# Turning x for layer 1: from TensorE and ScalarE to VectorE's 32x32 blocks and DMAs

## The chip, the cores and the metric

The kernel runs on one core of a Trainium2 chip. The metric is the device time of the whole kernel in microseconds, the median of several executions. Everything is float32.

## What is computed

The input x holds 128 graphs of 128 nodes with 512 features each, and adj is one 128x128 adjacency matrix. Four layers follow each other, and each one ends in a residual sum and a layer norm over the features:

```
layer 0:  x = LN(x + (adj x) W0 + bias)
layer 1:  q = x Wq', k = x Wk', v = x Wv'          (' is the transpose)
          rel = adj' * (q k')                      (* element by element, per graph)
          rel = rel / norm of its row
          x = LN(x + rel v)
layer 2:  h = x W;  e = leaky(s1 + s2') * adj;  att = softmax(e)
          x = LN(x + elu(att h + beta h))          (s1, s2: h times the two halves of a)
layer 3:  A = adj x;  C = adj x + b;  x = LN(x + max over n' of relu(A[.., n'] + C - A))
```

The change touches layer 1 only. There the kernel uses (x Wq')(x Wk')' = (x (Wq' Wk)) x': it makes the product matrix m_qk of the two weights once, then M = x m_qk and the scores M x' for each graph. TensorE contracts over the partitions (the 128 rows in which the on-chip memory is organised), so x has to lie with its features on the partitions and its nodes along the free dimension. After layer 0 it lies the other way round. The turned copy is called xT, and making it is what is changed.

## The kernel before, in words

**Groups and tiles.** The 128 graphs are taken in 32 groups of G = 4. For a group, x lies as [128 nodes, 4 graphs, 512 features] (x1 after layer 0, x2 after layer 1, x3 after layer 2). xT lies as [128, K = 4, 512]: feature k*128 + p on partition p, and the 4 x 128 nodes of the group along the free dimension.

**Products.** The four large products of a group (y with W0, m with m_qk, v with Wv', z with W2) are each a 512x512x512 product. `product` (L338) does it in seven steps on blocks of half size instead of eight, in the order 1, 2, 6, 5, 7, 3, 4 (L289). Some steps use sums and differences of blocks of the left factor. For m and v these are made by `left_factors` (L293) with four GpSimd instructions that read xT and write s_x. Each step is four matmuls of 128x256 in the program (eight records in the profile, since a float32 matmul is recorded as two), and its result leaves PSUM by a ScalarE copy or a VectorE addition. The profile calls the PSUM tiles of these steps r_y, r_m, r_v and r_z.

**Order of the work.** Nothing is left to a scheduler. Each piece of work is emitted at a due time from the table at L231: the number is a slot within the work of a group, group g is shifted by 28 slots, and all pieces are sorted by time (L757) and emitted; each engine then runs its instructions in that order. A group's pieces span some 130 slots, so that pieces of four to five groups stand side by side on every engine. What matters around the change, in slots of group g:

- 16.8 on: `norm`'s apply, ScalarE writes the normalised x1 of layer 0.
- 21.4, 22.4, 23.4, 24.4: `turn(b)` (L443), once for each graph. TensorE transposes four 128x128 blocks of x1 into a PSUM bank (p_xT), and ScalarE copies the bank into xT.
- 25.3 to 26.8: GpSimd makes the sums s_x from xT.
- 28 to 34: the seven steps of m. The first two read xT, the third reads a sum. M is written into the tile tT by ScalarE and VectorE.
- 36.5 to 39.5: `scores`, M times xT into p_rel.
- 39.95 to 41.5: `masked`, then `turn_rel` and `move_rel` (L489, L498): the masked scores are themselves turned by VectorE in blocks of 32x32 into relB, and 16 DMAs, 4 source quarters by 4 target quarters of the partitions, put the blocks in place in relT. VectorE's transpose turns each 32x32 block where it stands; exchanging the blocks across partitions is left to the DMAs.
- 42 to 48: the seven steps of v, of which the first, second and last read xT. Slot 48 is thus the last reader of xT, and falls on slot 20 of the next group. The tile xT has one buffer (tag aT_x).
- 50.6 on: `attend`, relT times v into p_o.

On TensorE, the turn of group g stands between the steps of z_w (r_z) of group g-2 and the `attend` matmuls of group g-1.

**Buffers.** The tiles tT (M), v and c (the result of z_w in layer 2) take turns in three buffers with the tag "nat". The same three hold the weights wq, wk and wv at the start.

**The DMA queue.** All DMAs of the loop are issued by SyncE in one order: for each group, the 16 DMAs of move_rel, four stores of the result of group g-3, and one load of x. The program rotates through eight semaphores for them, so a DMA waits until the one eight before it has landed.

Of the kernel before, what the change touches and what calls it, by code (L numbers as in the profile page):

```python
# [8 lines left out]
FP = mybir.dt.float32  # L9
# [20 lines left out]
def kernel(  # L30
# [33 lines left out]
    pe, dve, act, pool = (InOrder(tc, e) for e in (nc.tensor, nc.vector, nc.scalar, nc.gpsimd))  # L64
    sync = InOrder(tc, nc.sync)
    B, N, D = x.shape
    P = 128
    assert N == P and D % P == 0
    K = D // P
    Q = P // 32  # L70
    H = D // 2
    G = 4
# [5 lines left out]
    work = ctx.enter_context(tc.tile_pool(name="work", bufs=1))  # L78
# [3 lines left out]
    def bank(name):  # L82
        return psum.tile([P, D], FP, tag="ps", name=name)
# [8 lines left out]
    x1, x2, x3 = {}, {}, {}  # L92
# [12 lines left out]
    bias_sb = const.tile([P, D], FP)  # L105
    nc.scalar.dma_start(bias_sb, on_all(bias0, D))

    wq_sb = work.tile([P, K, D], FP, tag="nat", name="wq_sb", bufs=3)
    nc.sync.dma_start(wq_sb, wq.rearrange("(k p) f -> p k f", p=P))
    wk_sb = work.tile([P, K, D], FP, tag="nat", name="wk_sb", bufs=3)  # L110
    nc.sync.dma_start(wk_sb, wk.rearrange("(k p) f -> p k f", p=P))
    wv_sb = work.tile([P, K, D], FP, tag="nat", name="wv_sb", bufs=3)
    nc.sync.dma_start(wv_sb, wv.rearrange("(k p) f -> p k f", p=P))

    w2_sb = const.tile([P, K, D], FP)
# [104 lines left out]
    def emit(at, f, *args):  # L220
        pieces.append((at, lambda: f(*args)))

    def each(at, f):
        for b in range(len(at)):
            emit(at[b], f, b)

    def row(at, step, n=G):
        return [at + i * step for i in range(n)]
# [2 lines left out]
    TABLE = dict(  # L231
        load=[-20], y=row(0.5, 1), bias=row(1.3, 1), y_sums=row(5.2, 0.5), y_w=row(7, 1, 7),
        stats0=row(14.4, 0.4), norm0=[16.2], apply0=row(16.8, 0.33),
        turn=row(21.4, 1), x_sums=row(25.3, 0.5), m=row(28, 1, 7), scores=row(36.5, 1),
        masked=[39.95], squares=[40.4], turn_rel=[40.3],
        move_rel=row(41.2, 0.1), inverse=[42.5], v=row(42, 1, 7), attend=row(50.6, 1),
        residual=row(51.0, 1), dots=row(54.2, 1.1), norm1=[55.2], scale=[58.8],
# [6 lines left out]
        stats3=[99.8, 101.1, 104.7, 105.7], norm3=[106.2], apply3=row(107, 0.33), store=[108.5],  # L244
    )

    FIRST = {1: dict(y=row(-9.5, 0.3), bias=row(-9.2, 0.3))}

    LAST = {
        NG - 3: dict(  # L250
# [14 lines left out]
            m=[0.0, 1.73, 3.46, 5.2, 7.4, 9.1, 10.8], scores=row(12.7, 0.9), masked=[16.4],  # L265
# [16 lines left out]
    def times(g):  # L282
        t = {key: [28.0 * g + v for v in at] for key, at in TABLE.items()}
        t.update({key: [28.0 * g + v for v in at] for key, at in FIRST.get(g, {}).items()})
        t.update({key: [LAST_M + v / SLOT for v in at] for key, at in LAST.get(g, {}).items()})
# [7 lines left out]
    def left_factors(at, s, aT, tag, name, keep):  # L293

        def blk(nh, kh):
            return s[aT][:, 2 * kh : 2 * kh + 2, 2 * P * nh : 2 * P * (nh + 1)]

        def first():  # L300
            sums = work.tile([P, 3 + keep, 2, 2 * P], FP, tag=tag, name=f"s_{name}")
            s1, s2, s4 = (sums[:, i] for i in range(3))
            s3 = sums[:, 3] if keep else blk(1, 0)
            s["f"] = {1: blk(0, 0), 2: blk(0, 1), 3: s4, 4: blk(1, 1), 5: s1, 6: s2, 7: s3}
            pool.tensor_tensor(s1, blk(1, 0), blk(1, 1), ALU.add)

        emit(at[0], first)
        emit(at[1], lambda: pool.tensor_tensor(s["f"][6], s["f"][5], blk(0, 0), ALU.subtract))
        emit(at[2], lambda: pool.tensor_tensor(s["f"][7], blk(0, 0), blk(1, 0), ALU.subtract))
        emit(at[3], lambda: pool.tensor_tensor(s["f"][3], blk(0, 1), s["f"][6], ALU.subtract))  # L310
# [129 lines left out]
    def layer1(g, t):  # L440
        s = {}

        def turn(b):  # L443
            if b == 0:
                s["xT"] = work.tile([P, K, G * P], FP, tag="aT_x", name=f"xT_{g}")
            p = bank(f"p_xT_{g}_{b}")
            for k in range(K):
                pe.transpose(
                    p[:, k * P : (k + 1) * P], x1[g][:, b, k * P : (k + 1) * P], ident
                )  # L450
            act.copy(
                s["xT"][:, :, b * P : (b + 1) * P], p.rearrange("p (k n) -> p k n", k=K)
            )

        def begin_middle():
            s["tT"] = work.tile([P, K, G * P], FP, tag="nat", name=f"tT_{g}", bufs=3)

        def middle_block(nh, ch):
            return s["tT"][:, 2 * ch : 2 * ch + 2, 2 * P * nh : 2 * P * (nh + 1)]
# [48 lines left out]
            pool.tensor_tensor(s["rn"], s["n2"], mhalf, ALU.pow)  # L508

        def begin_values():  # L510
            s["v"] = work.tile([P, G, D], FP, tag="nat", name=f"v_{g}", bufs=3)

        def attend(b):
            s["o", b] = bank(f"p_o1_{g}_{b}")
# [37 lines left out]
        def scale_dots():  # L552
# [11 lines left out]
            )  # L564
            s12[g] = s["d"]

        each(t["turn"], turn)
        left_factors(t["x_sums"], s, "xT", "s_x", f"x_{g}", 1)
        product(t["m"], f"m_{g}", by_columns, s, "m", middle_block, True, begin_middle)
        each(t["scores"], scores)  # L570
        emit(t["masked"][0], masked)
        emit(t["squares"][0], squares)
        emit(t["turn_rel"][0], turn_rel)
        each(t["move_rel"], move_rel)
        emit(t["inverse"][0], inverse)
        product(t["v"], f"v_{g}", by_rows, s, "v", rows_of(lambda: s["v"]), True, begin_values)
        each(t["attend"], attend)
        each(t["residual"], residual)
# [9 lines left out]
    def layer2(g, t):  # L588
        s = {}
# [77 lines left out]
            )  # L667

        def begin():
            s["c"] = work.tile([P, G, D], FP, tag="nat", name=f"c_{g}", bufs=3)  # L670
            for b in range(G):
                s["c", b] = s["c"][:, b, :]

# [26 lines left out]
        n = G // len(t["exps"])  # L700
# [9 lines left out]
        if g < NG - 1:  # L710
            left_factors(t["z_sums"], s, "zT", "s_yz", f"z_{g}", 0)
            product(t["z_w"], f"z_{g}", by_rows, s, "2", rows_of(lambda: s["c"]), True, begin)
        else:
            each(t["z_w"], direct)
# [39 lines left out]
    for g in range(NG):  # L754
        for layer in (layer0, layer1, layer2, layer3):
            layer(g, times(g))
# [31 lines left out]
```

All engines are called through a helper (L26) that keeps program order, so that the profile puts nearly every instruction on line 26. The tile names tell them apart.

## Time and profile before

| | before |
|---|---|
| time, median of 3 | 2263.68 us (2263.55 to 2263.74) |
| span of the profiled execution | 2260.3 us |
| TensorE matmul, busy | 2221.2 us, 98% |
| VectorE, busy | 1599.1 us, 71% |
| ScalarE, busy | 1043.4 us, 46% |
| GpSimd, busy | 924.4 us, 41% |
| p_xT matmuls | 512, busy 76.1 us, mean 273 ns |
| copies p_xT to xT on ScalarE | 128, busy 74.5 us, mean 586 ns |
| TensorE clock granted | 0.996 |

The trace names an instruction by what it writes and reads: "p_xT<-ident,x" is a matmul into the PSUM tile p_xT from x and the identity matrix. A row of groups gives the instruction's count, its busy time, the mean duration of one in ns, and then the idle time of the engine just before such instructions with what ended it. A row of the timeline gives start, duration, engine, instruction and count; a bracket at its end is the idle time before it. PE is TensorE's matmul, PEld its loading of weights, DVE VectorE, ACT ScalarE, POOL GpSimd, SPq the queue of SyncE. Matmuls are pipelined, so their durations overlap, and what a matmul holds the engine for is the distance between two starts. A row of windows gives the busy time of each engine in a stretch, then the granted clock, the mean busy share of the 16 DMA engines and GB/s.

### The profile page before, as it was taken

How to read it: one execution, taken by the hardware profiler on the slowest of the kernel's cores; microseconds unless marked ns; L12 is line 12 of the kernel's file. 1: busy time of each engine (PE TensorE's matmuls, PEld its weight loads, DVE VectorE, ACT ScalarE, POOL GpSimd, SP SyncE). 2: the span in 40 equal slices, each digit the busy share in tenths (PEclk: the TensorE clock that was granted, in tenths of full speed). 3: DMA queues.
4: the chain of work that ended last, by engine and by line, in shares of the span. 5: the costliest groups of instructions: out<-in, count | busy, mean ns of one | idle time of the engine just before them, and what ended most of it. 6: DMA issues, size and time to landing. Idle time of an engine off the chain costs nothing.

```text
span 2260.3 us, 31788 instructions
## 1 busy us (share of the span) xinstructions
PE 2221.2 (98%) x11553; PEld 1884.2 (83%) x11553; DVE 1599.1 (71%) x3414; ACT 1043.4 (46%) x2056; POOL 924.4 (41%) x743
## 2 busy tenths in 40 slices
PE   7999999999999999999999999999999999999996
PEld 5888888888888888888888888888888888888873
DVE  4657776667766767766767766677767677667678
ACT  2235444454444454444454444544444544444545
POOL 3434444334444334444334443444443344443322
PEclk9999999999999999999999999999999999999998
DMA  4000111100111100111101111001111001110001
GB/s 164 24 24 9 40 39 42 43 24 25 43 38 43 42 24 25 41 40 43 43 12 37 39 42 43 24 24 43 38 43 43 25 24 42 39 43 24 15 15 56
DMA packets 79853, 83.67 MB, mean 37 GB/s; under 512 B 43985, under 2 KB 44113, under 8 KB 79697
## 3 DMA queue, kind: packets, MB, share of 16 engines
q1 hardware_dynamic: 78496, 79.28, 10.5%
q10 hardware_dynamic: 1200, 2.36, 0.3%
q8 instruction: 92, 1.51, 0.3%
q14 instruction: 65, 0.52, 0.1%
HBM read 39.65 MB, written 33.55 MB: 32 GB/s over the span
## 4 chain that ended last, share of the span: by engine, by line
PE 93%; DVE 4%; POOL 1%; ACT 1%; issue 1%; DMA 0%; ACTq 0%; DVEq 0%; POOLq 0%
PE r_y L26 17%; PE r_v L26 16%; PE r_m L26 16%; PE r_z L26 16%; PE p_rel L26 5%; PE p_z L26 5%; PE p_o L26 5%; PE p_y L26 5%; PE p_a L26 5%; PE p_xT L26 2%; DVE x L26 1%; DVE st L26 1%; PE p_eT L26 1%; PE p_m L26 1%; PE p_s L26 1%
## 5 line engine op out<-in xcount | busy, mean ns | idle before, releaser
L26 ACT ACTIVATE x<-x,nmean,rstd 128x512 f32<-128x512 f32 x512 | 389.0, 808 | 127.4 <-DVE nmean L26 127.2
L26 DVE BATCH_NORM_STATS2 st<-x 128x6 f32<-128x512 f32 x512 | 352.2, 688 | 74.8 <-ACT x L26 66.0
L26 POOL TENSOR_TENSOR rstd<-ve,mhalf 128x4 f32<-128x4 f32 (+1 forms) x134 | 144.5, 1078 | 360.0 <-DVE ve L26 356.0
L26 POOL TENSOR_TENSOR x<-x,bias_sb 128x512 f32<-128x512 f32 x128 | 173.9, 1361 | 146.5 <-PE p_y L26 146.5
L26 DVE SCALAR_TENSOR_TENSOR scr<-x,wa 128x512 f32<-128x512 f32 x256 | 214.4, 888 | 0.0
L26 ACT ACTIVATE x<-x,top 128x512 f32<-128x512 f32 x128 | 92.4, 722 | 225.3 <-DVE top L26 225.1
L26 DVE TENSOR_TENSOR v<-r_v,v 128x512 f32<-128x512 f32 x96 | 65.8, 685 | 178.5 <-PE r_v L26 175.5
L26 POOL TENSOR_TENSOR s_x<-xT 128x512 f32<-128x512 f32 x64 | 82.1, 1282 | 223.1 <-ACT xT L26 223.1
L26 DVE TENSOR_TENSOR x<-r_y,x 128x512 f32<-128x512 f32 x224 | 151.7, 678 | 30.2 <-PE r_y L26 29.8
L26 ACT COPY yT<-p_y 128x512 f32<-128x512 f32 x128 | 75.2, 587 | 205.7 <-PE p_y L26 205.7
L26 DVE SCALAR_TENSOR_TENSOR x<-p_o,rn,x 128x512 f32<-128x512 f32 x128 | 95.9, 749 | 100.0 <-PE p_o L26 97.1
L26 DVE SCALAR_TENSOR_TENSOR x<-m,x 128x512 f32<-128x512 f32 x128 | 114.8, 897 | 61.4 <-ACT m L26 51.4
L26 ACT COPY c<-r_z 128x512 f32<-128x512 f32 x124 | 72.7, 586 | 176.0 <-DVE scr L26 174.9
L26 PEld LDWEIGHTS p_y<-adjT,x 128*128 128x128 f32 x1024 | 135.0, 194 | 13.0 <-ACT adjT L26 5.1
L26 PE MATMUL p_y<-adjT,x 128*128 128x128 f32 x1024 | 135.8, 277 | 6.3 <-ACT adjT L26 4.8
L26 PEld LDWEIGHTS p_z<-eT,x 128*128 128x128 f32 x1024 | 133.9, 192 | 8.4 <-DVE x L26 1.2
L26 PEld LDWEIGHTS p_rel<-xT,tT 128*128 128x128 f32 x1024 | 134.1, 191 | 7.4 <-DVE tT L26 0.8
L26 PE MATMUL p_rel<-xT,tT 128*128 128x128 f32 x1024 | 134.9, 275 | 0.6 <-DVE tT L26 0.6
L26 PE MATMUL p_z<-eT,x 128*128 128x128 f32 x1024 | 134.8, 275 | 0.4 <-DVE x L26 0.4
L26 PE MATMUL p_a<-x,adjT 128*128 128x512 f32 x256 | 131.2, 597 | 3.6 <-ACT x L26 1.9
L26 ACT COPY tT<-r_m 128x512 f32<-128x512 f32 x128 | 75.7, 591 | 123.7 <-PE r_m L26 123.7
L26 POOL TENSOR_TENSOR s_z<-zT 128x512 f32<-128x512 f32 x31 | 39.2, 1263 | 225.7 <-ACT zT L26 225.7
(118 smaller groups left out, 5119.0 us busy)
## 6 DMA issues: line engine op xcount, KB each, us to landing
out_dram<-x SPq DMA_DIRECT2D x128, 256.0 KB, 2.0
x<-in_x_dram SPq DMA_DIRECT2D x31, 1024.0 KB, 5.3
relT<-relB SPq DMA_DIRECT2D x512, 16.0 KB, 1.8
w_sb<-in_L_gnn_weight_dram ACTq DMA_DIRECT2D x1, 1024.0 KB, 5.8
x<-in_x_dram SPq DMA_DIRECT2D x4, 256.0 KB, 7.7
wq_sb<-in_L_gnn_Wq_dram SPq DMA_DIRECT2D x1, 1024.0 KB, 12.2
wk_sb<-in_L_gnn_Wk_dram SPq DMA_DIRECT2D x1, 1024.0 KB, 14.9
w_sb<-in_L_gnn_W_dram ACTq DMA_DIRECT2D x1, 1024.0 KB, 10.1
```

The costliest lines, as they stand in the source:

```text
L26: return lambda *args, **kw: self.tc.keep_in_program_order(op(*args, **kw))
```

## The change

From the third group on, xT is made without TensorE and ScalarE. `turn_blocks(b)` at slots 18.4, 19.0, 19.6 and 20.2 turns one graph's x1 with one VectorE transpose in blocks of 32x32 into a new tile xB, laid out so that the values of one destination run are contiguous. `move(a)` at slots 20.5 to 20.8 issues 16 DMAs, each from 32 partitions of xB to 32 partitions of xT, in runs of 32 values, 128 bytes, 16 runs for each partition. The readers of xT (the sums, m, scores and v) are the same. It is for taking the transposes off TensorE. Groups 0 and 1 are turned as before, group 0 with its four pieces closer together.

xB needs a buffer of 8 KB a partition. It is found by letting M (tT) and v share one buffer (tag "tv"), with one buffer for c and one for xB: three in all, as before. The weights wq, wk and wv lie in these three at the start.

```diff
-    wq_sb = work.tile([P, K, D], FP, tag="nat", name="wq_sb", bufs=3)
+    wq_sb = work.tile([P, K, D], FP, tag="tv", name="wq_sb")
...
-        turn=row(21.4, 1), x_sums=row(25.3, 0.5), m=row(28, 1, 7), scores=row(36.5, 1),
+        turn=row(21.4, 1), turn_blocks=row(18.4, 0.6),
+        move=row(20.5, 0.1), x_sums=row(25.3, 0.5), m=row(28, 1, 7), scores=row(36.5, 1),
...
-    FIRST = {1: dict(y=row(-9.5, 0.3), bias=row(-9.2, 0.3))}
+    FIRST = {0: dict(turn=row(20.4, 0.3)), 1: dict(y=row(-9.5, 0.3), bias=row(-9.2, 0.3))}
...
+        def turn_blocks(b):
+            if b == 0:
+                s["xB"] = work.tile([P, Q, K, G, P // Q], FP, tag="xB", name=f"xB_{g}")
+                s["xT"] = work.tile([P, K, G * P], FP, tag="aT_x", name=f"xT_{g}")
+            dve.transpose(
+                s["xB"][:, :, :, b, :].rearrange("p q k u -> p k q u"),
+                x1[g][:, b, :].rearrange("p (k q u) -> p k q u", k=K, q=Q),
+            )
+
+        def move(a):
+            n = P // Q
+            for q in range(Q):
+                sync.dma_start(
+                    s["xT"][q * n : (q + 1) * n].rearrange("p k (b n) -> p (k b) n", b=G)[
+                        :, :, a * n : (a + 1) * n
+                    ],
+                    s["xB"][a * n : (a + 1) * n, q].rearrange("p k b n -> p (k b) n"),
+                )
...
-            s["tT"] = work.tile([P, K, G * P], FP, tag="nat", name=f"tT_{g}", bufs=3)
+            s["tT"] = work.tile([P, K, G * P], FP, tag="tv", name=f"tT_{g}")
...
-            s["v"] = work.tile([P, G, D], FP, tag="nat", name=f"v_{g}", bufs=3)
+            s["v"] = work.tile([P, G, D], FP, tag="tv", name=f"v_{g}")
...
-        each(t["turn"], turn)
+        if g < 2:
+            each(t["turn"], turn)
+        else:
+            each(t["turn_blocks"], turn_blocks)
+            each(t["move"], move)
...
-            s["c"] = work.tile([P, G, D], FP, tag="nat", name=f"c_{g}", bufs=3)
+            s["c"] = work.tile([P, G, D], FP, tag="c", name=f"c_{g}")
```

More of the change, by code (lines that the diff above doesn't have):

```diff
@@ L106 @@
     nc.scalar.dma_start(bias_sb, on_all(bias0, D))
-    wq_sb = work.tile([P, K, D], FP, tag="nat", name="wq_sb", bufs=3)
+    wq_sb = work.tile([P, K, D], FP, tag="tv", name="wq_sb")
     nc.sync.dma_start(wq_sb, wq.rearrange("(k p) f -> p k f", p=P))
-    wk_sb = work.tile([P, K, D], FP, tag="nat", name="wk_sb", bufs=3)
+    wk_sb = work.tile([P, K, D], FP, tag="c", name="wk_sb")
     nc.sync.dma_start(wk_sb, wk.rearrange("(k p) f -> p k f", p=P))
-    wv_sb = work.tile([P, K, D], FP, tag="nat", name="wv_sb", bufs=3)
+    wv_sb = work.tile([P, K, D], FP, tag="xB", name="wv_sb")
     nc.sync.dma_start(wv_sb, wv.rearrange("(k p) f -> p k f", p=P))
```

## The prediction

> **What bounds the kernel now.** I read the page's busy shares and its chain first, then the waits, then one group's timeline on TensorE and VectorE, last SyncE's queue and the DMA share.
>
> ```profile
> PE 2221.2 (98%) x11553; PEld 1884.2 (83%) x11553; DVE 1599.1 (71%) x3414; ACT 1043.4 (46%) x2056; POOL 924.4 (41%) x743
> ...
> PE 93%; DVE 4%; POOL 1%; ACT 1%; issue 1%; DMA 0%; ACTq 0%; DVEq 0%; POOLq 0%
> PE r_y L26 17%; PE r_v L26 16%; PE r_m L26 16%; PE r_z L26 16%; PE p_rel L26 5%; PE p_z L26 5%; PE p_o L26 5%; PE p_y L26 5%; PE p_a L26 5%; PE p_xT L26 2%; DVE x L26 1%; DVE st L26 1%; PE p_eT L26 1%; PE p_m L26 1%; PE p_s L26 1%
> ```
>
> The chain is TensorE for 93% of the span, and the turn of x (p_xT) is 2% of it. In the list of waits the longest entry of TensorE's matmuls is 4.8 us in total over the whole run. So time taken off TensorE comes back whole, unless something new makes TensorE wait. The chain's share is rounded; the timeline gives the price. On TensorE, a group in the middle of the run:
>
> ```profile
> 1039.28 1.89 PE L26 MATMUL r_v<-t_v,xT 128*128 128x256 f32 x8
> 1041.01 1.02 PE L26 MATMUL p_a<-x,adjT 128*128 128x512 f32 x2
> 1041.86 1.89 PE L26 MATMUL r_z<-w_sb,zT 128*128 128x256 f32 x8
> 1043.59 0.60 PE L26 MATMUL p_xT<-ident,x 128*128 128x128 f32 x4
> 1044.03 1.89 PE L26 MATMUL r_z<-w_sb,zT 128*128 128x256 f32 x8
> 1045.76 0.60 PE L26 MATMUL p_xT<-ident,x 128*128 128x128 f32 x4
> 1046.19 0.60 PE L26 MATMUL p_o<-v,relT 128*128 128x512 f32 x1
> ```
>
> The printed durations overlap, as matmuls are pipelined; what counts is start to next start. A block of four transposes holds TensorE from 1043.59 to 1044.03, 0.44 us.
>
> **What the Trainium skill says.** "TensorE: Matmul & The Clock Gate", Part 4 (PE-mode transpose), gives about 275 ns for a transpose in a kernel's context and says that the result lies in PSUM and has to be copied out. The trace agrees in both (273 ns mean for p_xT, and a ScalarE copy of 586 ns for each block), but the 273 ns is a latency: the spacing is 0.11 us. "VectorE: DVE Perf Modes", The three transpose paths, says that VectorE turns only 32x32 blocks, which is why DMAs must then put them in place, and it warns of plain DMAs that step through a transpose with a large innermost stride; here VectorE has made the innermost 32 values contiguous, so the warning is not this case. "DMA: Bandwidth & Descriptors" points two ways: its Specifications want at least 512 B for line rate, its section Why small descriptors are slow (HBM only) says that transfers within SBUF escape that, with 3 cycles of overhead for a packet: 11 cycles for 256 B. By that rule 128 B would be 128/32 + 3 = 7 cycles, an estimate. The trace of before has SBUF packets of 256 B and none of 128 B.
>
> **Removed.** For groups 2 to 31, 16 transposes on TensorE and 4 copies on ScalarE. TensorE: 4 blocks x 0.437 us = 1.75 us a group, x 30 groups = 52.4 us. ScalarE: 4 x 0.586 = 2.3 us a group; it is 46% busy and not on the chain, so I count 0. The four PSUM banks are freed too, worth 0 while nothing waits for banks.
>
> **Added on VectorE.** Four transposes of 128x512 a group. The row of the existing ones, 128x128, and of a pass over 128x512 in SBUF:
>
> ```profile
> L26 DVE STREAM_TRANSPOSE relB<-rel 128x128 f32<-128x128 f32 x128 | 28.7, 283 | 1.1
> ...
> L26 DVE BATCH_NORM_STATS2 st<-x 128x6 f32<-128x512 f32 x512 | 352.2, 688 | 74.8 <-ACT x L26 66.0
> ```
>
> A pass over 512 elements in SBUF takes 0.69 us (the statistics row), four times the small transpose 1.13 us; I take 0.7 us, as both are one pass over the tile. 4 x 0.7 = 2.8 us a group, at most 4.5. Do they fit? The instruction order of the changed program puts one ahead of the first v addition, two between the first and the second, one after "top". VectorE there:
>
> ```profile
> 1036.07 0.69 DVE L26 TENSOR_TENSOR v<-r_v,v 128x512 f32<-128x512 f32 x1 [3.91 <-PE r_v L26]
> 1038.62 0.69 DVE L26 TENSOR_TENSOR v<-r_v,v 128x512 f32<-128x512 f32 x1 [1.86 <-PE r_v L26]
> ...
> 1040.20 0.21 DVE L26 TENSOR_SCALAR top<-mx,b_sb 128x1 f32<-128x1 f32 x1
> 1041.27 0.69 DVE L26 BATCH_NORM_STATS2 st<-x 128x6 f32<-128x512 f32 x1 [0.85 <-ACT x L26]
> ```
>
> The brackets are idle time before the instruction: 3.91, 1.86 and 0.85 us, against 0.7, 1.4 and 0.7. They fit, and nothing queued behind them (the v additions, the statistics, the maxima) starts later. Cost 0. At 1.13 us each the second and third gap overrun by about 0.4 us, in a stretch where TensorE has no wait for VectorE; still 0 at first order. The last transpose ends at about 1041.1.
>
> **Added: the DMAs and the wait that replaces the copies.** Sixteen DMAs on SyncE's queue, each of 32 partitions x 16 runs of 128 B = 512 packets, 64 KB. The first may start only when its buffer is free: xT is single, and its last reader is r_v of the group before, which ends at 1041.01. So they start at about 1041.15, by TensorE and VectorE alike. TensorE needs all sixteen at the first r_m. It begins 18.15 us after the end of that r_v, 1059.16; less the 1.75 removed, 1057.4. The GpSimd sums s_x need them too, but r_m's first use of a sum is 5 us later and two sums take 2.6 us, so they tolerate a landing until about 1059.9. Window: 16.25 us. What is queued on SyncE behind the moves is four stores and one load with tens of us of slack. Is the window enough? The nearest thing measured is the move of the scores, also 16 DMAs from 32 partitions to 32 partitions in SBUF, 64 packets of 256 B each:
>
> ```profile
> 1021.71 10.18 SPq L26 DMA_DIRECT2D relT<-relB  x16
> ...
> relT<-relB SPq DMA_DIRECT2D x512, 16.0 KB, 1.8
> ...
> 1021.00:1032.00 11.00, 11.00 (x57) 9.17 (x56) 9.58 (x26) 5.59 (x16) 2.02 (x2) 1.00 0.10 22
> ...
> x<-in_x_dram SPq DMA_DIRECT2D x31, 1024.0 KB, 5.3
> ```
>
> First, issue. 10.18 / 16 = 0.64 us a DMA, set by the queue. Does issue grow with packets? The load of x is 512 packets in one DMA, and its issue takes 0.37 to 0.39 us on the queue's timeline. So it does not; I keep 0.64. Second, the engines. In the window row the DMA share is 0.10: 0.10 x 11 us x 16 engines = 17.6 us for 16 x 64 = 1024 packets, 17 ns a packet of 256 B. A 128 B packet lies between half of that, 8.5 ns, and all of it, 17 ns (the page's rule would make it 11). Sixteen moves are 8192 packets, 512 an engine: 4.4 to 8.7 us, all less than the issue, 10.2. So issue sets the pace: 15 x 0.64 + 2.0 for the last to land (1.8 for a small one, and the longer tail) = 11.6 us, landed at 1052.8. That is the time at which the fourth ScalarE copy ended before, and 4.6 us ahead of need. Cost 0. The bad end: if a 128 B packet cost two 256 B packets, 34 ns, 512 x 34 = 17.4, plus 2 = 19.4 us against 16.25: a stall of 3.2 us a group. The limit of "no stall" is 14.25 / 15 = 0.95 us a DMA; the gain is gone at (14.25 + 1.75) / 15 = 1.07 us.
>
> **The rest.** M and V in one buffer: V is first written when ScalarE copies r_v, 1024.70, after the scores read M, done by 1019; M of the next group is first written after 1060, after p_o has read V, done by 1056. Margins of over 4 us; cost 0. Group 0's turn emitted closer together and the weights in other buffers: only in the first 60 us; cost 0.
>
> **Sum.** 2263.7 - 52.4 + 0 = 2211.3 us.
>
> **Rivals.**
> 1. *DMAs too slow.* The r_m waits for the moves. With 34 ns a packet, a stall of 3.2 - 1.75 = 1.4 us net a group x 30 = +43: about 2307, slower than before. For: 245,760 packets of a size that no trace shows, the one page that asks for 512 B. Against: 17 ns at 256 B, and less to move per packet here.
> 2. *Gain partly eaten.* A pace of 1.0 us a DMA overruns by 15 x 0.05 = 0.75 us a group: 22 us back, 2234. For: issue of a pattern with sixteen short runs a partition is not measured either. Against: the load's issue of 0.38 us.
> 3. *Nothing left.* 1.07 us a DMA, or VectorE losing 1.75 us a group to TensorE's evacuations: 2264. Against: VectorE would rise only from 49.1 to 52 us in a group of 66.8, and the gaps are there.
>
> **How the numbers follow.** Forecast 0.70, rival 2 0.12, rival 3 0.04, rival 1 0.14. Faster by over 0.2%: 0.82; within: 0.04; slower: 0.14. Predicted 2211. The low end is 2205 (second-order help from free banks and ScalarE); the high end 2245 takes in most of rival 2 (up to 1.02 us a DMA). What is left out is rivals 1 and 3, some 0.2.
>
> **What would show it.** Right: no p_xT after the second group, group spacing 66.8 us in place of 68.6, moves issued at about 0.64 us, GpSimd's s_x released by a DMA at about the time it was released by the copy, and no wait of TensorE at r_m. Each step wrong: a list of waits with "r_m <- DMA", and then the queue's timeline says whether issue or packets set the pace; or VectorE's transposes well over 0.7 us and TensorE waiting for v or c. The prediction falls if the sixteen moves take over 16 us from first issue to last landing.

## The result, and the profile after

The changed kernel takes 2236.3 us (2235.4 to 2241.3) against 2263.6 us before (2263.3 to 2263.7): ratio 0.988, 95% interval 0.987 to 0.990. It is faster, but only by 27 us. The forecast was 52. The question is where the other 25 us went.

The page of the changed kernel: busy shares, the chain, the rows of VectorE's dot products (scr) and of GpSimd's sums, and the moves' row of DMA issues.

```profile
PE 2182.9 (98%) x11073; PEld 1842.1 (82%) x11073; DVE 1794.9 (80%) x3534; ACT 980.0 (44%) x1936; POOL 983.1 (44%) x743
...
PE 75%; DVE 20%; issue 3%; POOL 1%; ACT 1%; DMA 0%; DVEq 0%; ACTq 0%; POOLq 0%
...
L26 DVE SCALAR_TENSOR_TENSOR scr<-x,wa 128x512 f32<-128x512 f32 x256 | 286.2, 1169 | 0.0
...
L26 POOL TENSOR_TENSOR s_x<-xT 128x512 f32<-128x512 f32 x64 | 95.8, 1497 | 256.5 <-DMA xT<-xB 237.6
...
xT<-xB SPq DMA_DIRECT2D x480, 64.0 KB, 2.3
```

VectorE had 4% of the chain and now has 20%. It is busy for 196 us more (1794.9 against 1599.1), and the next lines show that the new transposes explain only 81 of them. The dots, which the diff does not touch, rose from 888 ns (214.4 us in all) to 1169 ns (286.2 us): 72 us. The first form of GpSimd's sums, also untouched, rose from 1282 ns to 1497 ns.

The new transposes, by shape, and then the waits that matter (waiting engine and tile, what it waits for: total us, times, longest):

```profile
L26 DVE STREAM_TRANSPOSE xB<-x 128x512 f32<-128x512 f32 x120 | 81.2, 696 | 38.6 <-ACT x L26 24.8 <-DMA relT<-relB 13.8
```
```profile
POOL s_x L26 <- DMA xT<-xB: 237.6, 29, 11.7
...
PE r_m L26 <- DVE tT L26: 6.8, 5, 1.7
...
PE r_y L26 <- DVE x L26: 4.4, 17, 0.4
```

In the loop no matmul waits for a DMA. TensorE waits for VectorE: r_m for the additions that build M, r_y for the additions x<-r_y,x that empty its PSUM tiles. The waits listed are short, 11.2 us in all, and do not add up to the 25 us, so the loss is better read from the distance between groups. From the start of one group's first r_m to the next it was 68.59 us in every group before. After, I sorted the groups of the trace (third to thirty-first) by that distance. "Lead" is how long before the first r_m the first sum s_x starts; "slow" counts those of VectorE's twelve instructions with both inputs in SBUF (eight dots, two x<-c,x and two x<-m,x, from 3 us before r_m to 20 us after) that took over 1 us instead of 0.68:

| | groups | lead, us | slow | first and second addition into M, us after r_m | distance, us |
|---|---|---|---|---|---|
| before | all | 6.0 | 3 | 5.5, 12.5 | 68.59 |
| after | 13 | 3.5 to 3.7 | 6 | 8.0 to 8.3, 12.5 | 66.81 |
| after | 8 | 3.3 to 3.5 | 7 | 8.3 to 8.5, 13.4 | 67.75 |
| after | 3 | 2.7 to 3.0 | 7 | 8.6 to 8.8, 13.6 | 67.9 to 68.2 |
| after | 4 | 2.2 to 2.5 | 8 to 9 | 9.0 to 9.3, 15.1 | 69.3 to 69.4 |
| after, the first with moves | 1 | 1.3 | - | - | 69.68 |

In 13 groups the whole forecast is there: 68.59 - 66.81 = 1.78 us. The others lose 8 x 0.94 + 3.7 + 10.0 + 2.9 = 24 us, which is the missing gain. The loss goes with the lead, and it goes in steps. In the eight groups that lose 0.94 us, TensorE loses nothing at r_m. Set beside a group without loss, it falls behind in r_y, 20.4, 28.3 and 30.5 us after r_m, and the wait that the trace names there is for x<-r_y,x. In the worst groups 1.5 us are lost at r_m and the rest in r_y.

Here is a group of the worst kind (r_m starts at 1046.32). First VectorE:

```profile
1044.68 1.08 DVE L26 SCALAR_TENSOR_TENSOR scr<-x,wa 128x512 f32<-128x512 f32 x1
...
1045.69 1.74 DVE L26 SCALAR_TENSOR_TENSOR scr<-x,wa 128x512 f32<-128x512 f32 x1
...
1049.12 1.75 DVE L26 SCALAR_TENSOR_TENSOR scr<-x,wa 128x512 f32<-128x512 f32 x1
...
1052.03 1.74 DVE L26 SCALAR_TENSOR_TENSOR scr<-x,wa 128x512 f32<-128x512 f32 x1
...
1053.70 1.75 DVE L26 SCALAR_TENSOR_TENSOR scr<-x,wa 128x512 f32<-128x512 f32 x1
...
1055.38 0.68 DVE L26 TENSOR_TENSOR tT<-r_m,tT 128x512 f32<-128x512 f32 x1
...
1057.06 1.81 DVE L26 SCALAR_TENSOR_TENSOR x<-c,x 128x512 f32<-128x512 f32 x1
1058.98 1.57 DVE L26 SCALAR_TENSOR_TENSOR x<-m,x 128x512 f32<-128x512 f32 x1
...
1061.40 0.67 DVE L26 TENSOR_TENSOR tT<-r_m,tT 128x512 f32<-128x512 f32 x1
```

Then GpSimd, and the matmul that waited for the second addition into M:

```profile
1043.95 1.27 POOL L26 TENSOR_TENSOR s_x<-xT 128x512 f32<-128x512 f32 x1 [8.92 <-DMA xT<-xB]
1045.29 1.60 POOL L26 TENSOR_TENSOR s_x<-s_x,xT 128x512 f32<-128x512 f32 x1
1046.85 1.73 POOL L26 TENSOR_TENSOR s_x<-xT 128x512 f32<-128x512 f32 x1
1048.53 1.79 POOL L26 TENSOR_TENSOR s_x<-xT,s_x 128x512 f32<-128x512 f32 x1
1050.28 1.46 POOL L26 TENSOR_TENSOR rstd<-ve,mhalf 128x4 f32<-128x4 f32 x1
1051.72 4.86 POOL L26 TENSOR_TENSOR x<-x,bias_sb 128x512 f32<-128x512 f32 x3
```
```profile
1062.13 1.99 PE L26 MATMUL r_m<-xT,t_m 128*128 128x256 f32 x8 [1.28 <-DVE tT L26]
```

And the same place before (r_m at 1059.16), GpSimd first:

```profile
1053.11 1.27 POOL L26 TENSOR_TENSOR s_x<-xT 128x512 f32<-128x512 f32 x1 [7.03 <-ACT xT L26]
...
1056.92 1.27 POOL L26 TENSOR_TENSOR s_x<-xT,s_x 128x512 f32<-128x512 f32 x1
```
```profile
1057.52 1.21 DVE L26 SCALAR_TENSOR_TENSOR scr<-x,wa 128x512 f32<-128x512 f32 x1
...
1058.66 0.68 DVE L26 SCALAR_TENSOR_TENSOR scr<-x,wa 128x512 f32<-128x512 f32 x1
```

Before, the four sums ended (1058.2) just as the dots began (1057.5), and met one of them. After, the sums start 2.4 us ahead of r_m and lie beside the dots. Each dot that meets one takes up to 1.75 us instead of 0.68, and the sums stretch too. GpSimd's next work, rstd, the additions of the bias and the sums s_y, then meets the later dots, x<-c,x and x<-m,x. VectorE runs in a fixed order, so the additions into M and the x<-r_y,x, which need no GpSimd, stand behind all that.

Most of the lost lead is the gain itself. Counted from the end of r_v, the sums start at 12.1 us before (1053.11 - 1041.01) and at 12.7 to 13.0 us after in most groups, so they are only 0.6 to 0.9 us later. But r_m, and the dots with it, starts at 16.38 us where it started at 18.15.

The steps can be read from one instruction, the first x<-m,x of a group. The last addition of the bias on GpSimd is released by TensorE, 10.72 us after r_m (11.03 in the first group with moves). First a group that loses nothing (r_m at 1519.50), then one that loses 0.94 us (r_m at 911.76):

```profile
1530.15 0.69 DVE L26 SCALAR_TENSOR_TENSOR x<-m,x 128x512 f32<-128x512 f32 x1
...
1530.22 1.75 POOL L26 TENSOR_TENSOR x<-x,bias_sb 128x512 f32<-128x512 f32 x1 [1.35 <-PE p_y L26]
```
```profile
922.48 1.27 POOL L26 TENSOR_TENSOR x<-x,bias_sb 128x512 f32<-128x512 f32 x1 [1.19 <-PE p_y L26]
...
922.57 1.74 DVE L26 SCALAR_TENSOR_TENSOR x<-m,x 128x512 f32<-128x512 f32 x1
```

The one that starts first runs its usual time, and the other pays. In the 13 groups without loss x<-m,x starts at most 0.003 us after that addition and takes 0.69 us. In the 16 others it starts at least 0.019 us after it and takes 1.56 to 1.80 us, and what follows on VectorE is late: the second addition into M comes at 13.4 us in place of 12.5. In the worst groups x<-c,x is already late enough to meet the addition (1057.06, 1.81 us), and x<-m,x meets the next sum as well. Before, x<-m,x starts 1.03 us ahead of the addition, and VectorE waits there for ScalarE. Stretched dots first use up this slack, and cost nothing until it is gone.

The Trainium skill names this: "SBUF — State Buffer", section Who interferes with whom, says that a VectorE instruction with two SBUF inputs contends with a GpSimd instruction that reads SBUF, that one with at most one SBUF input does not, and that the first to start keeps the shared ports for its whole instruction. The trace agrees: in the two pairs above the one that comes second pays, and for a dot 1.75 - 0.68 = 1.07 us is most of one 1.27 us sum. The additions into M read PSUM and one SBUF tile, and stay at 0.67 to 0.68 us in the worst group.

### The profile page after: what moved, and what is told of

Read it like the earlier page. It is cut to its first block, busy times and chain, and to the rows that moved or that the text cites. A ratio compares the mean times of both kernels' runs of the same rounds, so it can differ in the third digit from the quotient of the medians.

```text
span 2234.4 us, 31661 instructions
## 1 busy us (share of the span) xinstructions
PE 2182.9 (98%) x11073; PEld 1842.1 (82%) x11073; DVE 1794.9 (80%) x3534; ACT 980.0 (44%) x1936; POOL 983.1 (44%) x743
## 3 DMA queue, kind: packets, MB, share of 16 engines
q1 hardware_dynamic: 331936, 110.77, 19.6%
## 4 chain that ended last, share of the span: by engine, by line
PE 75%; DVE 20%; issue 3%; POOL 1%; ACT 1%; DMA 0%; DVEq 0%; ACTq 0%; POOLq 0%
PE r_v L26 17%; PE r_y L26 15%; PE r_z L26 14%; PE r_m L26 8%; DVE scr L26 6%; DVE x L26 6%; PE p_z L26 5%; PE p_o L26 5%; PE p_a L26 5%; PE p_rel L26 4%; DVE st L26 2%; PE p_y L26 2%; DVE tT L26 1%; DVE d L26 1%; PE p_m L26 1%
## 5 line engine op out<-in xcount | busy, mean ns | idle before, releaser
L26 DVE SCALAR_TENSOR_TENSOR scr<-x,wa 128x512 f32<-128x512 f32 x256 | 286.2, 1169 | 0.0
L26 POOL TENSOR_TENSOR x<-x,bias_sb 128x512 f32<-128x512 f32 x128 | 193.2, 1519 | 76.9 <-PE p_y L26 76.4
L26 POOL TENSOR_TENSOR s_x<-xT 128x512 f32<-128x512 f32 x64 | 95.8, 1497 | 256.5 <-DMA xT<-xB 237.6
L26 DVE SCALAR_TENSOR_TENSOR x<-m,x 128x512 f32<-128x512 f32 x128 | 129.7, 1013 | 13.6 <-DVE x L26 0.9
L26 PE MATMUL p_o<-v,relT 128*128 128x512 f32 x256 | 130.3, 593 | 0.0
## 6 DMA issues: line engine op xcount, KB each, us to landing
wq_sb<-in_L_gnn_Wq_dram SPq DMA_DIRECT2D x1, 1024.0 KB, 12.1
```

The lines of the kernel that those rows point to most:

```text
L26: return lambda *args, **kw: self.tc.keep_in_program_order(op(*args, **kw))
```

## The experiments

The theory, A: the sums start too late, fall beside VectorE's instructions with two SBUF inputs, and both stretch. Rivals: B, the added transposes are too much for VectorE. C, the traffic of the moves slows the engines or the other DMAs. D, the moves are late by themselves or through other DMAs. E, GpSimd's lateness costs by itself, through the work queued behind the sums, without a collision. Each ratio below is to the kernel before as timed beside that run (2262.2 to 2262.5 us).

### 1. Sums that do not wait for the moves

The four sums read xB, the tile ahead of the moves, so they start some 11 us ahead of r_m; the values of M and V are then not those of the reference. All else is as in the changed kernel.

```diff
+        def unmoved(nh, kh):
+            return s["xB"][:, :, 2 * kh : 2 * kh + 2, 2 * nh : 2 * nh + 2, :].rearrange(
+                "p q k b n -> p q k (b n)"
+            )
...
-            pool.tensor_tensor(s1, blk(1, 0), blk(1, 1), ALU.add)
...
+                s["u"], s["w"] = unmoved, shaped
...
+            pool.tensor_tensor(s["w"](s1), s["u"](1, 0), s["u"](1, 1), ALU.add)
```

> The changed kernel, but GpSimd's four sums read xB, the blocks before the DMAs move them, so they need not wait for the DMAs (the sums then stand in the wrong places, so M and V are wrong; all else is as in the changed kernel). Theory A (collision: the late sums run beside VectorE's instructions with two SBUF inputs, both are stretched, and TensorE waits for VectorE's additions): the lost 27 us come back, 2209 to 2214 us, and the dots (scr) fall from a mean of 1169 ns to below 900. Theory B (VectorE's four added transposes are what is too much): no change, 2236. Theory C (the traffic of the DMAs slows the engines): no change, 2236.

Measured: 2210.3 us, ratio 0.977 (0.976 to 0.978). All groups from the third on at 66.81 us. The chain and the dots of this kernel:

```profile
PE 93%; DVE 4%; POOL 1%; ACT 1%; issue 1%; DMA 0%; ACTq 0%; DVEq 0%; POOLq 0%
```
```profile
L26 DVE SCALAR_TENSOR_TENSOR scr<-x,wa 128x512 f32<-128x512 f32 x256 | 198.0, 829 | 0.0
```

With every transpose and every move in place, the whole forecast comes out once the sums are early. That speaks against B and C, and leaves A and E.

### 2. No transposes on VectorE

VectorE's transposes are left out and xB is filled once with a constant, so xT holds that constant.

```diff
-            dve.transpose(
-                s["xB"][:, :, :, b, :].rearrange("p q k u -> p k q u"),
-                x1[g][:, b, :].rearrange("p (k q u) -> p k q u", k=K, q=Q),
-            )
...
+                if not blank:
+                    blank.append(work.tile([P, Q, K, G, P // Q], FP, tag="xB", name="xB_once"))
+                    dve.memset(blank[0], 0.5)
+                s["xB"] = blank[0]
```

> The changed kernel with VectorE's four transposes a group left out: xB is filled once and the DMAs move that (xT is wrong). Theory A: still about 2233 to 2238 us, with the dots still stretched, since the sums still wait for the DMAs. Theory B: 2211. Theory C: 2236.

Measured: 2240.2 us, ratio 0.990 (0.988 to 0.993), a little above what I expected; dots 1180 ns. Without 81 us of work on VectorE the time is no better. B falls.

### 3. The kernel before, with late sums

Only the sums are delayed: a tiny GpSimd instruction ahead of them reads the last x2 of the group before, so that they start 2.3 us ahead of r_m.

```diff
+            if keep and g > 0:
+                hold = small.tile([P, 1], FP, tag="hold", name=f"hold_{name}")
+                pool.tensor_tensor(hold, x2[g - 1][:, 3, 0:1], x2[g - 1][:, 3, 1:2], ALU.add)
             pool.tensor_tensor(s1, blk(1, 0), blk(1, 1), ALU.add)
...
-        turn=row(21.4, 1), x_sums=row(25.3, 0.5), m=row(28, 1, 7), scores=row(36.5, 1),
+        turn=row(21.4, 1), x_sums=row(26.1, 0.25), m=row(28, 1, 7), scores=row(36.5, 1),
```

> The kernel before, with its transposes on TensorE, where one small GpSimd instruction that reads x2 of the last graph holds the four sums back until about 2.3 us ahead of r_m, the distance they have in the changed kernel; before, it was 6 us. Nothing is added to VectorE or the DMAs. Theory A: slower than before by 20 to 30 us, 2284 to 2294, with the dots stretched as in the changed kernel. Theories B and C: 2264 to 2266.

Measured: 2337.2 us, ratio 1.033 (1.032 to 1.035). Its dots, and two waits of TensorE:

```profile
L26 DVE SCALAR_TENSOR_TENSOR scr<-x,wa 128x512 f32<-128x512 f32 x256 | 308.9, 1257 | 0.0
```
```profile
PE r_m L26 <- DVE tT L26: 34.4, 27, 1.3
...
PE r_y L26 <- DVE x L26: 8.9, 31, 1.3
```

The direction is A's; the size is far above what I had expected, because I had scaled from the changed kernel's average, where few groups have so short a lead. Group by group it fits: 71.1 us, 2.5 us more than 68.59, with a lead of 2.3 us; the changed kernel's groups with 2.2 to 2.5 us of lead stand at 69.3, 2.5 us more than 66.81. The additions into M fall at 9.2 and 15.1 us after r_m in both. So lateness of the sums alone, with none of the change in the program, makes the loss.

### 4. The kernel before, with a middle lead

The same with x2 of the third graph instead of the last, which gives a lead of 4.9 us.

```diff
-                pool.tensor_tensor(hold, x2[g - 1][:, 3, 0:1], x2[g - 1][:, 3, 1:2], ALU.add)
+                pool.tensor_tensor(hold, x2[g - 1][:, 2, 0:1], x2[g - 1][:, 2, 1:2], ALU.add)
```

> The kernel before with the sums held until the residual of the third graph in place of the fourth, so that they start about 4.9 us ahead of r_m (6.0 before, 2.3 when held for the fourth). Theory A with the limit that the groups of the changed kernel show, about 3.5 us: no loss, 2262 to 2266. If every us of delay costs its share (2337 - 2262 over 3.7 us of delay): 2262 + 75 x 1.1 / 3.7, about 2284.

Measured: 2266.7 us, ratio 1.0016 (1.0009 to 1.0023): groups at 68.59 but for two, an early one and one at 69.56. Losing 1.1 us of the 6.0 us of lead costs next to nothing, losing 3.7 us costs 2.5 us a group. There is slack, and then a step. The dots take 1130 ns here, nearly as long as in the changed kernel (1169), so stretched dots alone are not the loss. The group at 69.56 has the same lead, 4.9 us, as its neighbours without loss; in it VectorE stood idle for 0.39 us ahead of x<-c,x, and x<-m,x then started 0.27 us after the last addition of the bias. So the lead sets the loss only through that order.

### 5. The kernel before, with everything added and nobody waiting

Transposes into xB, 480 moves of the same form (x1 to xB, 128-byte runs) and the shared buffer of M and V are added; the turn by TensorE and ScalarE stays and feeds xT.

```diff
         each(t["turn"], turn)
+        if g >= 2:
+            each(t["turn_blocks"], turn_blocks)
+            each(t["move"], move)
```

> The kernel before with everything that the change adds and nobody waiting for it: xT is made by TensorE and ScalarE, and from the third group on VectorE's four transposes write xB and 16 DMAs of 64 KB in runs of 128 bytes follow, from x1 into xB, read by nobody; M and V share a buffer. Theory A: 2264 to 2267 us, as the sums start when they did before. Theory B: 2285 or more. Theory C: 2285 or more.

Measured: 2263.1 us, ratio 1.0002 (0.9994 to 1.0011). Its page:

```profile
PE 2223.8 (98%) x11553; PEld 1886.6 (83%) x11553; DVE 1674.8 (74%) x3534; ACT 1044.1 (46%) x2056; POOL 925.9 (41%) x743
...
PE 94%; DVE 3%; POOL 1%; ACT 1%; issue 0%; DMA 0%; ACTq 0%; DVEq 0%; POOLq 0%
```

VectorE carries 76 us more, the DMAs 31 MB more, and the time is the same. The moves need not wait for the end of r_v here and run some 7 us earlier than in the changed kernel; experiment 1 has them at their own time, and loses nothing either. B and C are out: what was added costs nothing; the wait for it costs.

### 6. Dots that read one SBUF input

In the changed kernel the dots with wa are replaced by plain sums of x2 (a tensor_reduce of the same 128x512), so the attention's terms s1 and s2 are not those of the reference. The sums s_x stay as late as they are.

```diff
-                dve.scalar_tensor_tensor(
-                    scr,
-                    x2[g][:, b, :],
-                    1.0,
-                    wa[:, i, :],
...
-                )
+                dve.tensor_reduce(s["d"][:, i, b : b + 1], x2[g][:, b, :], AX.X, ALU.add)
```

> The changed kernel with the eight dots of a group (VectorE, two SBUF inputs, x2 times wa with a sum) replaced by eight plain sums of x2 over the same 128x512, one SBUF input (the weights wa are left out, so the output is wrong). The sums of GpSimd start as late as in the changed kernel. Theory A (VectorE and GpSimd stretch each other where both read two SBUF inputs): the stretch goes, four sums take 5.1 us again in place of 6.0 to 6.6, groups are at 66.8 us, 2207 to 2214. Rival E (GpSimd's own lateness: what comes behind the sums on GpSimd is late for TensorE): the late groups still take 68 to 69 us, 2225 to 2236.

Measured: 2207.1 us, ratio 0.975 (0.974 to 0.977), all groups at 66.81. Dots and sums in this kernel:

```profile
L26 DVE TENSOR_REDUCE d<-x 128x1 f32<-128x512 f32 x256 | 156.5, 670 | 0.0
...
L26 POOL TENSOR_TENSOR s_x<-xT 128x512 f32<-128x512 f32 x64 | 82.3, 1287 | 260.0 <-DMA xT<-xB 249.2 <-ACT xT L26 10.9
```

The sums wait for the moves as long as ever (249.2 us), start up to 14.6 us after the end of r_v, and nothing is lost. They end up to 4.2 us after r_m starts, while the changed kernel loses in groups whose sums end at 2.5 us. A dot with one input takes 0.67 us, about what an undisturbed dot with two takes (0.68), and a sum is back at 1.29 us. So the loss is the collision, not the lateness: E falls, A holds.

### 7. Stores out of the way

The last move often lands a little later than its issue explains. D's simplest form is that the four stores issued right behind it (L231, store) take the DMA engines. Here they are issued 17.3 slots later, after the DMAs of the masked scores, and, as a control, the same in the kernel before.

```diff
-        stats3=[99.8, 101.1, 104.7, 105.7], norm3=[106.2], apply3=row(107, 0.33), store=[108.5],
+        stats3=[99.8, 101.1, 104.7, 105.7], norm3=[106.2], apply3=row(107, 0.33), store=[125.8],
```

> The changed kernel with one due time moved: the four stores of a group are issued after the DMAs of the masked scores in place of right after the moves of x, so that no store shares the DMA engines with the last move. In the changed kernel the last 128-byte run of a group lands 12.1 us after the end of r_v where it is undisturbed and 12.9 to 13.4 us where it meets a store, and those are the groups of 69.3 us; groups whose sums start by 12.9 us take 66.8. Theory A: every group's sums start by 12.9 us, all groups take 66.8 to 67.0 us, 2209 to 2214 us. If the sums are too late even without the stores (rival D: the DMAs themselves take too long): still 2225 or more.

> Control: the kernel before with its stores moved to the same later time. Nothing waits for a store there: 2262 to 2265 us, no change, under every theory. If it is faster by itself, the gain of the late stores is not the collision with the moves.

Measured: 2238.9 us, ratio 0.989 (0.987 to 0.990); the control 2263.9 us, 1.0002 (0.9993 to 1.001). My expectation fell: the stores do not delay the moves. The trace says what does. Counted from the end of r_v, the sixteenth issue ends at 10.9 us and its data land at 12.1 us in most groups. GpSimd then still takes four wait instructions for eight semaphores in a fixed order, about 0.09 us each; the last move's semaphore is another one in each group, so the sums start between 12.66 and 13.02 us. In five groups of the changed kernel the last data land at 12.9 to 13.4 us, and just before, at 11.4 to 11.8 us, a packet of 16 KB of the instruction queue begins, about 1 us long. In three more the sixteenth issue is late, at 11.5 to 11.8 us, because one issue took 1.3 to 1.5 us; in each of them such a packet began at 4.6 to 4.9 us. The edge between loss and no loss is at 12.92 us, where one group lost and another did not, so that most groups pass or fail by a tenth of a microsecond. This part is read from the trace; no run removed the instruction packets.

### 8. Issuing from two queues

If the pace of sixteen issues on one queue sets how late the sums are, two queues should mend it. ScalarE issues four of the sixteen moves, or two, and SyncE the rest. Nothing is left out in these kernels.

```diff
-        def move(a):
+        def move(a, qs=range(Q), queue=sync):
...
-            each(t["move"], move)
+            emit(28.0 * g + 20.45, move, 3, (0, 1, 2, 3), act)
+            each(t["move"][:3], move)
```

> Changed kernel, with the four moves of the last source quarter issued by ScalarE and the other twelve by SyncE, so that two queues issue side by side. Theory A (the sums come too late and run beside VectorE's dots; the pace of sixteen issues on one queue sets how late): the last data land at about 9.5 us after the end of r_v instead of 12.1, the sums start at about 10.3 us, some 6 us ahead of r_m as in the kernel before, a margin of 2.6 us over the 3.5 us at which the stretch set in, enough for the groups that a 1 us instruction fetch delays: all groups at 66.8 us, 2209 to 2214 us. Rival: ScalarE loses four issues, some 2.5 us, in a stretch where it copies r_v and p_a, VectorE and TensorE wait for it, and the time is 2220 us or more. If lateness of the sums is not the cause: 2236 us as the changed kernel.

> As the run with four moves on ScalarE, with two only. Theory A: landing 1.3 us earlier, the sums start at about 11.6 us after the end of r_v, a lead of about 4.7 us; groups that an instruction fetch delays by 1 us have 3.7 us, just above the 3.5 us limit: 2209 to 2216 us, a few groups at most over 67 us. Rival (ScalarE's issues cost TensorE): half the loss of the run with four. If lateness is not the cause: 2236 us.

Measured: 2211.9 us with four (ratio 0.978, 0.976 to 0.979) and 2212.1 us with two (0.978, 0.977 to 0.979). Both beat the kernel before and the changed one. With four on ScalarE, the chain, both queues at one group, and the dots:

```profile
PE 93%; DVE 4%; POOL 1%; ACT 1%; issue 1%; DMA 0%; ACTq 0%; DVEq 0%; POOLq 0%
```
```profile
1019.59 8.77 SPq L26 DMA_DIRECT2D xT<-xB  x12
```
```profile
1019.56 3.22 ACTq L26 DMA_DIRECT2D xT<-xB  x4
1022.82 0.59 ACT L26 COPY v<-r_v 128x512 f32<-128x512 f32 x1 [3.23 <-DMA xT<-xB]
```
```profile
L26 DVE SCALAR_TENSOR_TENSOR scr<-x,wa 128x512 f32<-128x512 f32 x256 | 233.5, 963 | 0.0
```

The last data land at about 10.05 us instead of 12.1, the sums lead by 4.5 to 6.1 us, and the groups stand at 66.8 to 67.0 us. ScalarE is held for 3.2 us at v<-r_v, and that shows only as the 0.1 to 0.2 us in some groups. With two, landing is at 10.8 to 11.1 us and the lead 4 to 5 us in most groups; one group has 3.3 us, and it is the only one that loses, 68.03. That is the edge of the table once more. The dots of this kernel take 1131 ns, and it loses almost nothing. In the Trainium skill, "DMA: Bandwidth & Descriptors", section Issuing engines are not separate DMA queues, says that a second issuing engine saves only its time on the sequencer; here the sequencer's time was what counted, 2.1 us of it.

| kernel | us | lead, us | dots, ns |
|---|---|---|---|
| before | 2263.6 | 6.0 | 888 |
| changed | 2236.3 | 1.3 to 3.7 | 1169 |
| sums do not wait | 2210.3 | about 11 | 829 |
| no transposes | 2240.2 | as changed | 1180 |
| before, late sums | 2337.2 | 2.3 | 1257 |
| before, middle lead | 2266.7 | 4.9 | 1130 |
| before, all added, unused | 2263.1 | 6.0 | 890 |
| one-input dots | 2207.1 | as changed | 670 |
| late stores | 2238.9 | as changed | 1172 |
| four moves on ScalarE | 2211.9 | 4.5 to 6.1 | 963 |
| two moves on ScalarE | 2212.1 | 3.3 to 5.0 | 1131 |

One reading of the traces holds throughout. The changed kernel and the six runs in which sums are late or wait for moves and the dots have both inputs (experiments 2, 3, 4, the late stores of 7, and both of 8) have 203 groups from the third to the thirty-first. The 87 that lose over 0.3 us are exactly those in which the first x<-m,x starts 0.006 us or more after the last addition of the bias. In the other 116 it starts ahead of it, or within 0.003 us of it.

## Why the prediction was wrong, point by point

- *TensorE, 1.75 us a group.* Right: 1.78 us in the undisturbed groups, and 2262.3 - 2211.9 = 50.4 us of the 52.4 in the kernel with four moves on ScalarE, against the kernel before timed beside it.
- *VectorE's transposes, 0.7 us, in gaps.* Right: 696 ns, and the run that adds them with no one waiting stays at 2263.1 us.
- *The moves.* Nearly right. SyncE's queue and a stretch of ten microseconds within it:

```profile
1030.17 10.66 SPq L26 DMA_DIRECT2D xT<-xB  x16
```
```profile
1031.00:1041.00 10.00, 10.00 (x42) 7.71 (x41) 6.49 (x15) 5.24 (x8) 1.57 (x2) 1.00 0.59 94
```

  10.66 / 16 = 0.67 us a DMA against 0.64 forecast. 94 GB/s x 10 us / 128 B = 7340 packets in 0.59 x 10 x 16 = 94 us: 12.9 ns a packet, inside the 8.5 to 17. Last data 12.1 us after the end of r_v against 11.75.
- *No wait of TensorE at r_m for the moves.* Right: no such entry. r_m starts 16.38 us after the end of r_v, 16.4 forecast.
- *M and V in one buffer, the rest: 0.* Right, by the same run with all added.
- *The sums: "so they tolerate a landing until about 1059.9 ... landed at 1052.8 ... Cost 0".* This is the step that failed. I reckoned the sums' slack to their reader on TensorE alone, and it is true that r_m never waits for s_x in the middle of the run. What ends first is the slack to VectorE: the sums stretch the dots that they meet, and in the changed kernel the lead must stay above about 3.5 us so that x<-m,x still comes ahead of the last addition of the bias. I counted that r_m moves 1.75 us towards the landing, but not that the dots move with it. My own figures had the landing 4.6 us ahead of r_m, so even they left only about 1 us, where I thought I had 7. The moves' 0.35 us and the semaphore waits of 0.5 to 0.9 us, which I had not priced, used that up. The term I had at 0 is 25 us.
- *The rivals.* Rival 2 named 2234 us, close to what came, for a cause that did not occur: a pace of 1.0 us a DMA with TensorE waiting for a DMA. The pace was 0.67. That 2236 us lies inside my range is luck, since the high end stood for that rival. Rival 3 mentioned VectorE losing time to TensorE's evacuations (the instructions that empty PSUM: the additions into M, x<-r_y,x), which is the place of the loss, but I dismissed it with VectorE's sum of work. The sum was not the matter; the durations changed.

What stays open: the order of x<-m,x and the last addition of the bias separates the groups without an exception, but it is read from traces; no run moved that pair alone. How a delay of about 1 us on VectorE becomes just 0.94 us on TensorE was not followed step by step.

## What to carry to other kernels

When a producer gets later, ask not only whether its reader still gets the data in time, but beside what the readers' work now runs: a GpSimd instruction that reads SBUF and a VectorE instruction with two SBUF inputs cost each other most of an instruction when they meet. Such a pair of streams can have a phase that keeps them mostly apart, and the profile of before shows it only as durations near their minimum (dots at 888 ns, 680 alone). Work taken off the bottleneck changes that phase by itself: what is tied to the bottleneck comes earlier, and what waits for something else does not. A mean duration that rises in a row that the diff does not touch is the first sign, though not yet a loss (at 1130 ns two kernels lost next to nothing); then add the new work without its wait, and the wait without the new work.

## What the runs showed of the hardware

- A VectorE dot over 128x512 with two SBUF inputs takes 0.68 us alone and up to 1.75 us beside GpSimd's SBUF reads; GpSimd's 1.27 us addition becomes 1.6 to 1.8 us. Of two that meet, the second to start pays: with x<-m,x first 0.69 and 1.75 us, with GpSimd first 1.74 and 1.27 us. With one input VectorE takes 0.67 us in the same place, and GpSimd 1.29 us.
- SBUF to SBUF runs of 128 B cost about 12.9 ns each on a DMA engine, and a DMA of 512 of them is issued at 0.67 us, nearly as one of 64 packets (0.64 us).
- From the last data of sixteen moves to GpSimd's first sum it takes 0.5 to 0.9 us in undisturbed groups (up to 1.2 in the others), with eight semaphores waited for in a fixed order.
- Packets of 16 KB of the instruction queue take about 1 us each. In the five groups of the changed kernel where one began at 11.4 to 11.8 us after the end of r_v, the last of sixteen moves landed 0.8 to 1.2 us later than elsewhere.
